# Graph-attention sums in six banks: wide products, a split pair end and values made one tile at a time

## The chip, the cores and the metric

The kernel runs on one NeuronCore of one Trainium2 chip. The metric is the device time in microseconds (us) of one execution; most executions of one kernel agree within 0.3%. The time before is 3559.61 us, median of 3 runs (3555.86 to 3563.96). A run is called slow when it is over 1.5% above the fastest of its kernel; none told of here is.

## The reference, cut to what matters

4096 nodes with 256 features pass two graph-attention layers and then one masked transformer layer. Only the graph-attention layers are touched:

```python
def _gat_layer(x, adj_mat, W, a):                 # 8 heads of 32
    Wh = jnp.einsum('nd,hdo->hno', x, W)
    src = jnp.einsum('hno,ho->hn', Wh, a[:, :O])
    dst = jnp.einsum('hno,ho->hn', Wh, a[:, O:])
    e = jax.nn.leaky_relu(src[:, :, None] + dst[:, None, :], 0.2)
    e = jnp.where(adj_mat[None, :, :] > 0, e, NEG_INF)
    alpha = jax.nn.softmax(e, axis=-1)
    return jnp.einsum('hnm,hmo->hno', alpha, Wh)   # then transposed and reshaped
```

The exponential of a leaky ReLU of a sum is one of two products, depending on the sign of the sum. So the kernel needs no exponential per edge. It compares (a 0/1 matrix `t8` per head, already ANDed with the mask) and sums two kinds of value rows: with `t8`, and with the mask alone.

## The kernel before

Work goes by layer, block of node tiles (4, 4, 8, 8, 8 tiles of 128 nodes in layer 0, then 8, 8, 8, 8), pair of heads (4) and group of sources (8 groups of 4 tiles). The code numbers the source groups by `q` and calls them quarters, though there are eight. Each value is held as two float16 halves, a high and a low one. `V1` is 33 (32 features and the denominator), `VW` 66, `SW` 198. A node tile needs 198 columns: 66 for each head and 66 for the mask. The sums are added up in PSUM, the memory that TensorE writes, of which the kernel uses eight banks. Two tiles share a bank, so eight tiles take four banks; two more are the buffer `two` for the values, and two are `turn` banks.

```python
for n in range(TILES[l][nb]):
    w, at = n // per, slice(n % per * P, (n % per + 1) * P)
    sums = acc[n // 2][:, n % 2 * SW : (n % 2 + 1) * SW]
    for m in range(G):
        for j in range(2):                 # head
            for k in range(2):             # high half, low half, onto the same 66 columns
                nc.tensor.matmul(sums[:, j * VW : (j + 1) * VW], t8[:, j, w, m, at],
                                 vst[g][:, m, 2 * p + j, k * VW : (k + 1) * VW], ...)
        for k in range(2):                 # mask, both heads
            nc.tensor.matmul(sums[:, 2 * VW :]..., masks[l, nb][g][:, w, m, at],
                             vst[g][:, m, 2 * p : 2 * p + 2, k * VW + V1 : (k + 1) * VW], ...)
    if g == NG - 1 and n % 2 == 1:
        nc.scalar.copy(ev[:, n - 1 : n + 1]..., acc[n // 2][:, : 2 * SW])
# ... (cut)
def values(l, q, half):                    # two node tiles at a time
    pv = two_banks()                       # one buffer of two banks
    # ... 4 float32 matmuls; negd, r, tops; for i in range(2): exp, product, high half, low half
```

In the profiles TensorE is PE, and its weight loads are PEld. ScalarE (ACT) and VectorE (DVE) share the comparisons, DVE does the AND. `compare` for group i + 2 is issued before the matmuls of group i. In layer 0, `mask_turn` also reads rows of the adjacency matrix into one of three row buffers (`g_rows`), converts them on DVE (`adj_bf`), transposes them on TensorE into a `turn` bank and copies them out on ACT. `features` loads rows of x into the same `g_rows` buffers and transposes them through `turn` too.

Of the kernel before, what the change touches and what calls it, by code (L numbers as in the profile page):

```python
# [8 lines left out]
F32 = mybir.dt.float32  # L9
# [6 lines left out]
AF = mybir.ActivationFunctionType  # L16
ALU = mybir.AluOpType
AX = mybir.AxisListType
# [3 lines left out]
P = 128  # L22
BIG = 2.0**100
LRELU = 0.2
# [657 lines left out]
VALUE_MAX = 12.0  # L682
# [66 lines left out]
def graph_attention(  # L749
# [16 lines left out]



    nc = tc.nc
    N = adj.shape[0]  # L770
    H, D, O = weights[0][0].shape
# [10 lines left out]
    NG = NT // G  # L782
    V1 = O + 1
    VW = 2 * V1
    SW = 3 * VW

    dram = ctx.enter_context(tc.tile_pool(name="g_dram", bufs=1, space=DRAM))
    s_d = [dram.tile([H, N], F32, name=f"s_d{l}") for l in range(NL)]
# [14 lines left out]
    make_identity(nc, ident_f)  # L803

    vst = [keep.tile([P, G, H, 2 * VW], F16, name=f"vst{q}") for q in range(NG)]

    def two_banks():
        return ps.tile([P, 2, 512], F32, name="two")

    def turn_bank(shape, dtype):  # L810
        return ps.tile(shape, dtype, name="turn", tag="turn", bufs=2)
# [66 lines left out]
    for l, (w, a) in enumerate(weights):  # L878
        L = Layer()
        L.w_ext = keep.tile([P, DC, D + 2 * H], F32, name=f"g_w_ext{l}")  # L880
        for c in range(DC):
            nc.sync.dma_start(
                L.w_ext[:, c, 0:D].rearrange("p (h o) -> p h o", o=O),
                w[:, c * P : (c + 1) * P, :].rearrange("h p o -> p h o"),
            )
        a_sb = rows_p.tile([P, H, 2, O], F32, name="g_rows")
        nc.sync.dma_start(
            a_sb.rearrange("p h s o -> p (h s o)"), spread(a, [[0, P], [1, H * 2 * O]])
        )
        wa = rows_p.tile([P, H, O], F32, name="g_rows")  # L890
        for c in range(DC):
            for s in range(2):
                nc.vector.tensor_tensor(
                    wa,
                    L.w_ext[:, c, 0:D].rearrange("p (h o) -> p h o", o=O),
                    a_sb[:, :, s, :],
                    op=ALU.mult,
                )
                nc.vector.tensor_reduce(
                    L.w_ext[:, c, D + s * H : D + (s + 1) * H], wa, AX.X, ALU.add  # L900
                )
        L.negd = keep.tile([P, NT, H], F32, name=f"g_negd{l}")
        L.r = keep.tile([P, NT, H], F32, name=f"g_r{l}")
        L.tops = keep.tile([P, NG, 2], F32, name=f"g_tops{l}")
        L.ft = {}
        layers.append(L)

# [14 lines left out]
    def term_rows(l, q):  # L922

        L = layers[l]
        pr = turn_bank([P, HB], F32)
        for c in range(DC):
            nc.tensor.matmul(
                pr[:H, :],
                L.w_ext[:, c, D : D + H],
                L.ft[q][:, c, :],  # L930
                start=(c == 0),
                stop=(c == DC - 1),
            )
        sr = rows_p.tile([H, HB], F32, name="g_rows")
        nc.scalar.copy(sr, pr[:H, :])
        nc.sync.dma_start(s_d[l][:, q * HB : (q + 1) * HB], sr)

    def values(l, q, half):

        L = layers[l]  # L940
        pv = two_banks()
        for i in range(2):
            t = 2 * half + i
            for c in range(DC):
                nc.tensor.matmul(  # L945
                    pv[:, i, : D + 2 * H],
                    L.ft[q][:, c, t * P : (t + 1) * P],
                    L.w_ext[:, c, :],
                    start=(c == 0),
                    stop=(c == DC - 1),  # L950
                )
        at = slice(G * q + 2 * half, G * q + 2 * half + 2)
        nc.vector.tensor_scalar(
            L.negd[:, at, :], pv[:, :, D + H : D + 2 * H], -1.0, None, op0=ALU.mult
        )
        nc.scalar.activation(L.r[:, at, :], pv[:, :, D : D + H], AF.Exp, scale=LRELU - 1.0)
        nc.vector.tensor_reduce(
            L.tops[:, q, half : half + 1], pv[:, :, :D], AX.XY, ALU.max, apply_absolute_value=True
        )
        heads = vst[q][:, 2 * half : 2 * half + 2].rearrange("p t h v -> p (t h) v")  # L960
        for i in range(2):

            big = some.tile([P, 2, H], F32, name="g_big")
            nc.scalar.activation(big, L.negd[:, at, :], AF.Exp, scale=(-1.0, -LRELU)[i])
            prod = some.tile([P, 2, H, V1], F32, name="g_prod")
            nc.vector.tensor_scalar(prod[:, :, :, O], big, UP, None, op0=ALU.mult)
            nc.vector.tensor_tensor(
                prod[:, :, :, :O],
                pv[:, :, :D].rearrange("p t (h o) -> p t h o", o=O),
                prod[:, :, :, O : O + 1].to_broadcast([P, 2, H, O]),  # L970
                op=ALU.mult,
            )
            part = prod.rearrange("p t h v -> p (t h) v")
            high = heads[:, :, i * V1 : (i + 1) * V1]
            low = heads[:, :, VW + i * V1 : VW + (i + 1) * V1]
            nc.scalar.copy(high, part)
            nc.vector.tensor_tensor(low, part, high, op=ALU.subtract)

    def check_values(l):
        L = layers[l]  # L980
        for values_, bound in (
            (L.tops.rearrange("p q t -> p (q t)"), VALUE_MAX),
            (L.negd.rearrange("p t h -> p (t h)"), DST_MAX),
            (L.r.rearrange("p t h -> p (t h)"), R_MAX),
        ):
            checks.below(some, values_, bound)

    def preparation(l, q):

        steps = [lambda: (term_rows(l, q), values(l, q, 0)), lambda: values(l, q, 1)]  # L990
        if q + 1 < NG:
            steps.insert(0, lambda: features(l, q + 1))
        else:
            steps.append(lambda: check_values(l))
        return steps
# [39 lines left out]
    def pair_end(l, nb, p, ev):  # L1035
# [5 lines left out]
        cols = slice(2 * p * O, (2 * p + 2) * O)  # L1041
        held = {}
        wide = [P, n, 2, V1]

        def block(name, last):
            return ep.tile([P, BT, 2, last], F32, name=name)[:, :n]

        def sums(i):

            return ev[:, :n, 0 : 2 * VW].rearrange("p t (j v) -> p t j v", j=2)[  # L1050
                :, :, :, i * V1 : (i + 1) * V1
            ]

        def step_load():
            held["x"] = block("e_x", O)
# [1 line left out]

        def step_sum():
            y = block("e_y", V1)
            over = ev[:, :n, 2 * VW :].rearrange("p t (j v) -> p t j v", j=2)  # L1060
            nc.vector.tensor_tensor(y, over, sums(1), op=ALU.subtract)
            nc.vector.tensor_tensor(  # L1062
                y, y, L.r[:, at, 2 * p : 2 * p + 2].unsqueeze(3).to_broadcast(wide), op=ALU.mult
            )
            nc.vector.tensor_tensor(y, y, sums(0), op=ALU.add)
            held["y"] = y

        def step_divide():
# [87 lines left out]
    for i, (l, nb, p, g) in enumerate(groups):  # L1156
# [30 lines left out]
        if not (i + 2 < len(groups) and groups[i + 2][1:] in ((0, 0, 0), (0, 0, 1))):  # L1187
            prepare(i + 2)
        t8 = s8.pop(i)
        if g == 0:  # L1190
            acc = [
                ps.tile([P, 512], F32, name=f"bank{k}") for k in range(TILES[l][nb] // 2)
            ]
        if g == NG - 1:
            ev = ep.tile([P, BT, SW], F32, name="ev")
        for n in range(TILES[l][nb]):
            w, at = n // per, slice(n % per * P, (n % per + 1) * P)
            sums = acc[n // 2][:, n % 2 * SW : (n % 2 + 1) * SW]
            for m in range(G):
                first, last = g == 0 and m == 0 and n % 2 == 0, g == NG - 1 and m == G - 1  # L1200
                for j in range(2):
                    for k in range(2):
                        nc.tensor.matmul(  # L1203
                            sums[:, j * VW : (j + 1) * VW],
                            t8[:, j, w, m, at],
                            vst[g][:, m, 2 * p + j, k * VW : (k + 1) * VW],
                            start=first and j == 0 and k == 0,
                            stop=False,
                        )
                for k in range(2):  # L1210
                    nc.tensor.matmul(  # L1211
                        sums[:, 2 * VW :].rearrange("p (j v) -> p j v", j=2),
                        masks[l, nb][g][:, w, m, at],
                        vst[g][:, m, 2 * p : 2 * p + 2, k * VW + V1 : (k + 1) * VW],
                        start=False,
                        stop=last and k == 1 and n % 2 == 1,
                    )
            if g == NG - 1 and n % 2 == 1:
                nc.scalar.copy(
                    ev[:, n - 1 : n + 1].rearrange("p t v -> p (t v)"), acc[n // 2][:, : 2 * SW]  # L1220
                )
            if slots:
                slots.pop(0)()
        while slots:
# [508 lines left out]
```

## Time and profile before

| stretch (from the first sum matmul of a pair of heads to that of the next) | us |
|---|---|
| until the first sum matmul | 47.4 |
| first pair of layer 0 (makes five of eight quarters of the values) | 81.9 |
| the other 7 four-tile pairs | 213.3 |
| layer 0, blocks 2 and 3 (8 pairs, with mask turns) | 429.8 |
| layer 0, last block (4 pairs; holds the start of layer 1) | 230.0 |
| first pair of layer 1 | 86.1 |
| the other 15 pairs of layer 1 | 732.4 |
| end of the graph layers | 1820.8 |
| transformer | 1741 |

The cuts are read from the start times of the sum matmuls in the trace; the graph layers end with the last of them. A clean pair is a pair of eight tiles beside which neither mask tiles are turned nor values made. A "unit" is what one node tile does with one 128-row of sources; 256 units make a pair of eight tiles. A step is the time from one matmul's start to the next one's start. The lines behind the table are shown in the prediction. One more matters for what follows. It is the view of the sums' banks: what had the matmuls idle before them (us, times).

```profile
its engine sat idle before it (us, times) until:
  PE bank L1211: 25.1, 9
  issue: 23.5, 28
  ACT ev L1219: 7.0, 6
```

"Issue" is time in which an engine waited for nothing that the profile shows: 28 waits before sum matmuls, 23.5 us.

### The profile page before, as it was taken

To read this page: it belongs to the slowest core of one execution; us is meant where nothing else is said; L and a number is where in the kernel's file an instruction comes from. 1 tells how busy PE (TensorE), PEld (TensorE's weight loads), DVE (VectorE), ACT (ScalarE), POOL (GpSimd) and SP (SyncE) were. 2 spreads that over 40 slices of the span, in tenths; PEclk is the share of its full clock that TensorE was granted. 3 is DMA by queue.
4 is the path that set the end of the run, shared out by engine and by line. 5 is a ranking of instruction groups with operands and counts; after the bars stand their busy time and mean duration, and the time that the engine had idled before them with its cause. 6 is when DMAs were issued, how large, how long until landed. Compare 5 with 4: busy or idle time off the path is not lost.

```text
span 3561.9 us, 131329 instructions
## 1 busy us (share of the span) xinstructions
PE 3392.7 (95%) x60099; PEld 2180.5 (61%) x60099; DVE 2857.7 (80%) x3344; ACT 2681.5 (75%) x3176; POOL 1239.4 (35%) x538
## 2 busy tenths in 40 slices
PE   7898999999989999999987999999999999997998
PEld 5898999999969999999964111111111111122666
DVE  7999788888798888888852999999999999996111
ACT  5899898988668888888854777777777777775332
POOL 0000000000000000000000999999999999996110
PEclk9999999999999999999998999999999999998999
DMA  5566554531211212111147010101010110002110
GB/s 174 169 195 210 160 163 135 160 102 39 75 50 37 83 40 75 39 57 46 28 103 194 13 43 16 40 13 37 19 31 25 25 36 13 25 10 69 42 48 25
DMA packets 199685, 254.84 MB, mean 72 GB/s; under 512 B 88080, under 2 KB 134672, under 8 KB 199120
## 3 DMA queue, kind: packets, MB, share of 16 engines
q1 hardware_dynamic: 199120, 246.34, 23.1%
q8 instruction: 472, 7.73, 0.9%
q14 instruction: 93, 0.76, 0.1%
HBM read 203.83 MB, written 42.47 MB: 69 GB/s over the span
## 4 chain that ended last, share of the span: by engine, by line
PE 77%; DVE 8%; ACT 7%; issue 3%; POOL 2%; DMA 2%; SPq 0%; DVEq 0%; ACTq 0%; POOLq 0%
PE bank L1203 26%; PE bank L1211 13%; PE u_ps L1452 11%; PE u_av L1466 11%; PE u_dn L1466 5%; DVE u_e L1461 4%; ACT t L1025 3%; PE misc L1638 3%; POOL u_both L1552 2%; PE misc L1391 2%; ACT u_ps L1459 1%; PE two L945 1%; PE misc L1622 1%; ACT stage L851 1%; PE turn L850 1%
## 5 line engine op out<-in xcount | busy, mean ns | idle before, releaser
L1203 PE MATMUL bank<-vst,t 128*128 128x66 f16 x32768 | 1567.9, 194 | 29.2 <-issue 15.2
L1203 PEld LDWEIGHTS <-t 128*128 128x128 fp8e4 x32768 | 1554.3, 98 | 38.5 <-issue 30.0
L1211 PE MATMUL bank<-vst,mask 128*128 128x66 f16 x16384 | 1554.6, 193 | 8.5 <-issue 8.3
L1025 ACT ACTIVATE t<-s_b,g_negd 128x1024 int8<-128x1024 f32 (+1 forms) x1296 | 1266.2, 1048 | 212.4 <-PE bank L1203 198.5
L1552 POOL TENSOR_TENSOR u_both<-u_e 128x1024 f32<-128x1024 f32 x512 | 1200.2, 2369 | 241.1 <-DVE u_e L1461 240.9
L1461 DVE SCALAR_TENSOR_TENSOR u_e<-u_mask,u_ps 128x1024 f32<-128x1024 uint8 x1024 | 1201.7, 1215 | 100.8 <-ACT u_ps L1459 95.5
L1459 ACT ACTIVATE u_ps<-u_ps 128x1024 f32<-128x1024 f32 x1024 | 1010.7, 1008 | 296.0 <-PE u_ps L1452 277.0
L1211 PEld LDWEIGHTS <-mask 128*128 128x128 fp8e4 x16384 | 1048.8, 97 | 11.1 <-issue 10.2
L1030 DVE TENSOR_TENSOR t<-t,mask 128x2048 int32<-128x2048 int32 (+1 forms) x288 | 590.7, 2052 | 210.9 <-ACT t L1025 204.8
L1027 DVE TENSOR_SCALAR t<-s_b,g_negd 128x1024 fp8e4<-128x1024 f32 (+1 forms) x1008 | 635.3, 688 | 10.1 <-PE bank L1203 9.3
masks.py:197 POOL MEMSET u_ident<- 128x128 f32 x1 | 0.2, 205 | 1821.5 <-DVE e_y L1062 1821.5
L1452 PE MATMUL u_ps<-u_q,u_k 128*128 128x512 f16 x2048 | 580.3, 384 | 36.8 <-DMA u_q<-half_d 21.6
L1452 PEld LDWEIGHTS <-u_k 128*128 128x128 f16 x2048 | 139.3, 97 | 743.7 <-issue 685.4
L1466 PE MATMUL u_av<-u_e,u_v 128*32 128x512 f32 x4096 | 547.2, 605 | 0.1
L1466 PE MATMUL u_dn<-u_both,u_ones 128*32 128x512 f32 x2048 | 274.0, 605 | 1.3 <-POOL u_both L1552 1.3
L1466 PEld LDWEIGHTS u_av<-u_e,u_v 128*32 128x32 f32 x4096 | 80.8, 108 | 219.2 <-issue 211.0
L1629 ACT ACTIVATE u_hid<-misc,u_b 128x512 f32<-128x512 f32 x64 | 42.4, 684 | 142.7 <-PE misc L1622 142.7
L851 ACT ACTIVATE stage<-turn 128x1024 fp8e4<-128x1024 bf16 x112 | 112.2, 1018 | 0.0
L1645 DVE TENSOR_TENSOR u_xres<-u_xres,misc 128x256 f32<-128x256 f32 x32 | 13.5, 421 | 122.7 <-PE misc L1638 122.7
L1638 PE MATMUL misc<-u_w,u_hid 128*128 128x256 f32 x512 | 111.8, 379 | 0.0
L1622 PE MATMUL misc<-ln_cols,u_w 128*128 128x512 f32 x256 | 111.2, 592 | 0.0
L1466 PEld LDWEIGHTS u_dn<-u_both,u_ones 128*32 128x32 f32 x2048 | 40.6, 108 | 110.9 <-issue 108.4
(100 smaller groups left out, 1565.9 us busy)
## 6 DMA issues: line engine op xcount, KB each, us to landing
g_rows<-in_adj_dram SPq DMA_DIRECT2D x128, 512.0 KB
mask<-mask SPq DMA_DIRECT2D x120, 256.0 KB
s_b<-s_d SPq DMA_DIRECT2D x56, 512.0 KB
u_mask<-mask SPq DMA_DIRECT2D x32, 512.0 KB
mask<-stage SPq DMA_DIRECT2D x28, 512.0 KB
half_d<-u_halves SPq DMA_DIRECT2D x32, 256.0 KB
u_k<-half_d SPq DMA_DIRECT2D x32, 256.0 KB
u_q<-half_d SPq DMA_DIRECT2D x32, 256.0 KB
```

The source lines that it names most:

```text
L851: nc.scalar.activation(staged[0].rearrange("p i g n -> p (i g) n")[:, :, t * P : (t + 1) * P], pt, AF.Identity, saturate=False,)
L1025: nc.scalar.activation(to.bitcast(I8), s, AF.Sign, bias=negd, scale=-1.0)
L1027: nc.vector.tensor_scalar(to, s, negd, None, op0=ALU.is_ge, saturate=False)
L1030: nc.vector.tensor_tensor(both, both, mask.unsqueeze(1).to_broadcast(list(both.shape)), op=ALU.bitwise_and)
L1203: nc.tensor.matmul(sums[:, j * VW : (j + 1) * VW], t8[:, j, w, m, at], vst[g][:, m, 2 * p + j, k * VW : (k + 1) * VW], start=first and j = ...
L1211: nc.tensor.matmul(sums[:, 2 * VW :].rearrange("p (j v) -> p j v", j=2), masks[l, nb][g][:, w, m, at], vst[g][:, m, 2 * p : 2 * p + 2, k * ...
L1452: nc.tensor.matmul(ps[:, j, :], k_st[:, h, mt * P : (mt + 1) * P], q_st[:, h, :], start=True, stop=True,)
L1459: nc.scalar.activation(ps, ps, AF.Exp, scale=SCALE)
L1461: nc.vector.scalar_tensor_tensor(e, mask, 0.0, ps, op0=ALU.not_equal, op1=ALU.mult)
L1466: nc.tensor.matmul(to[j * O : (j + 1) * O, :], lefts[j], es[j // 2][:, j % 2, :], start=start, stop=stop,)
L1552: nc.gpsimd.tensor_tensor(both, es_of[i - 1][u], es_of[i][u], op=ALU.add)
L1638: nc.tensor.matmul(po[:, :D], hid[:, f, at : at + P], w2_sb[:, f, :], start=(f == 0), stop=(f == FC - 1),)
```

## The change

The intent is fewer matmul instructions for the same columns. The two halves of the first head are no longer added in PSUM but stand side by side, as do those of the mask: 132 columns in one matmul. The second head still adds in place (two of 66). So a unit is 132, 66, 66, 132 and no longer six times 66. A tile now needs 330 columns, eight tiles six banks, and the value buffer loses its two: values are made one tile at a time in the `turn` banks. The pair end has to add the halves.

```diff
-    def values(l, q, half):
+    def values(l, q, t):
-        pv = two_banks()
+        pv = turn_bank([P, 512], F32)
... (the same steps for one tile; both products in one operation)
         def step_sum():
+            halves = ev[0][:, : 2 * n]
+            nc.vector.tensor_tensor(
+                halves[:, :, :VW], halves[:, :, :VW], halves[:, :, VW:], op=ALU.add
+            )
... (one subtraction and one addition of 528 become two each of 264)
-            acc = [ps.tile([P, 512], F32, name=f"bank{k}") for k in range(TILES[l][nb] // 2)]
+            banks = -(-2 * tiles // 3)
+            acc = [ps.tile([P, 512], F32, name=f"bank{k}") for k in range(banks)]
... (places: three wide sums and one narrow one to a bank)
+                todo = [
+                    (k_0, acc[k_0][:, o_0 : o_0 + 2 * VW], s_of_m[0], heads[:, 0, :]),
+                    (k_1, acc[k_1][:, o_1 : o_1 + VW], s_of_m[1], heads[:, 1, :VW]),
+                    (k_1, acc[k_1][:, o_1 : o_1 + VW], s_of_m[1], heads[:, 1, VW:]),
+                    (k_m, acc[k_m][:, o_m : o_m + 2 * VW]..., masks[l, nb][g][:, w, m, at], over),
+                ]
... (two copies a bank: wide sums to ev_broad, narrow ones to ev_narrow)
```

## The prediction

> **What bounds the kernel now.** I read the page first (who is busy, what the chain is made of), then the groups by line, then the busy time of each engine in stretches cut at the points where one pair of heads ends and the next begins, and last the matmuls one by one.
>
> ```profile
> span 3561.9 us, 131329 instructions
> ...
> PE 3392.7 (95%) x60099; PEld 2180.5 (61%) x60099; DVE 2857.7 (80%) x3344; ACT 2681.5 (75%) x3176; POOL 1239.4 (35%) x538
> ...
> PE bank L1203 26%; PE bank L1211 13%; PE u_ps L1452 11%; PE u_av L1466 11%; PE u_dn L1466 5%; DVE u_e L1461 4%; ACT t L1025 3%; PE misc L1638 3%; POOL u_both L1552 2%; PE misc L1391 2%; ACT u_ps L1459 1%; PE two L945 1%; PE misc L1622 1%; ACT stage L851 1%; PE turn L850 1%
> ...
> L1203 PE MATMUL bank<-vst,t 128*128 128x66 f16 x32768 | 1567.9, 194 | 29.2 <-issue 15.2
> ...
> L1211 PE MATMUL bank<-vst,mask 128*128 128x66 f16 x16384 | 1554.6, 193 | 8.5 <-issue 8.3
> ```
>
> The chain of waits puts 26% + 13% = 39% of the span (1389 us) on the two matmul lines that the change touches. All of that lies in the two graph-attention layers, which end at 1821 us (start of the last L1203 matmul); the transformer after it, 1741 us, is not touched. 1389 us / 49152 = 28.3 ns, but the chain leaves pieces out; the stretches give a better figure. In them each engine has its busy time and its count of instructions:
>
> ```profile
> 820.50:868.70 48.20, 48.20 (x1541) 48.20 (x1538) 41.34 (x47) 40.23 (x42) 0.00 (x0) 1.00 0.12 36
> ...
> 669.30:721.90 52.60, 52.42 (x1613) 52.32 (x1611) 47.02 (x57) 48.83 (x52) 0.00 (x0) 1.00 0.51 162
> 247.50:279.00 31.50, 29.84 (x850) 28.97 (x850) 28.64 (x56) 31.43 (x49) 0.00 (x0) 1.00 0.79 259
> 1002.40:1088.50 86.10, 81.08 (x1663) 68.18 (x1662) 77.33 (x132) 61.86 (x107) 0.00 (x0) 1.00 0.09 28
> ```
>
> The columns are length, PE, PEld, DVE, ACT, POOL, granted clock, DMA. Four kinds of stretch:
> - A clean pair of heads in a block of eight node tiles (first line): PE never idles, 1536 sum matmuls in 48.2 us. DVE 41.3, ACT 40.2. PE-bound. Of 36 pairs, 19 are like this or nearly: four in layer 0's last block, 15 in layer 1. Cut in the same way, the 15 last 48.2 to 51.1 us, so about 0.4 us each is lost to other waits (most of it named "issue").
> - Layer 0's blocks 2 and 3 (second line), which also turn mask tiles: 8 pairs of 50.5 to 60.4 us. PE has 48.1 us of sums and 72 transposes of 56 ns, ACT 48.8.
> - Four-tile pairs (third line), 7 of them, about 26 to 32 us: ACT 31.4 of 31.5. ACT-bound; PE has only 24.1 us of sums.
> - The first pair of each layer (fourth line), where values are made: DVE 77.3 of 86.1.
>
> Matmul by matmul in a clean pair:
>
> ```profile
> 1399.81 0.29 PE L1203 MATMUL bank<-vst,t 128*128 128x66 f16 x4
> 1399.94 0.22 PE L1211 MATMUL bank<-vst,mask 128*128 128x66 f16 x2
> 1400.00 0.29 PE L1203 MATMUL bank<-vst,t 128*128 128x66 f16 x4
> 1400.13 0.22 PE L1211 MATMUL bank<-vst,mask 128*128 128x66 f16 x2
> 1400.19 0.29 PE L1203 MATMUL bank<-vst,t 128*128 128x66 f16 x4
> ```
>
> One unit (a node tile by one 128-row of sources) repeats every 0.19 us. From the start times in the trace its six steps are 29, 34, 33, 32, 30 and 30 ns (medians over layer 1), together 188. 256 units make 48.1 us.
>
> **What the Trainium skill says.** (1) "TensorE: Matmul & The Clock Gate", section "Back-to-back issue gap": a warm isolated gap is about N/2.4 + 2.5 ns. For 66 columns that is 30.0 and the mask matmuls step by 30; for 128 it is 55.8 and the mask transposes step by 56; for 512 it is 215.8 and L1452's shortest steps are 215 to 216. The trace agrees. The same section's ~81 ns for a stream of load and matmul at 128 does not show here. (2) "PSUM — Partial Sum Buffer", section "The four PSUM rules": a first matmul clears the accumulate bits of the whole bank, so a bank may be opened only once; the changed code opens each once. No run here shows it yet. (3) "VectorE: DVE Perf Modes", section "The TRN2 errata": a float32 tensor_tensor takes (N+151)/0.96 ns. For 528 that is 707 and for 264 432; the e_y rows have 702 to 707 and 426 to 430. Agrees, so I use it for the new sizes.
>
> **The change, part by part.**
>
> *Sums.* Per unit six matmuls of 66 columns become 132, 66, 66, 132. Columns stay at 396, so only the fixed part of two matmuls goes. By N/2.4 + 2.5: 2 x 57.5 + 2 x 30 = 175 ns. Today's unit is 8 ns above its own 180 (the steps around matmuls of a head's own products, 32 to 34); I keep half of that, as half of those matmuls remain narrow: 179. Saved 188 - 179 = 9 ns a unit, 256 x 9 = 2.3 us a clean pair (48.1 to 45.8). Over all 8192 units 74 us, if PE were the bound everywhere.
>
> *Evacuation.* Eight tiles: four copies of 396 (483 ns each, 1.93 us) become five of 396, one of 132, five of 66, one of 198. From 483 ns for 396 and 372 for 256 (another copy row) the slope is 0.8 and the fixed part near 0.16: 5 x 0.483 + 0.26 + 5 x 0.21 + 0.32 = 4.05 us. ACT +2.1 us a pair; for four tiles +1.05.
>
> *Pair end.* Three DVE operations of 528 (2.1 us) become one of 1056 ((1056+151)/0.96 = 1.26 us), four of 264 (0.43 each) and one of 528 (0.71): 3.7 us. DVE +1.6 us; four tiles +1.0.
>
> *Values by one tile.* Per two tiles DVE had 0.17 + 0.69 + 2 x (0.17 + 0.68 + 0.70) = 4.0 us; now twice (0.15 + 0.42 + 0.32 + 0.68 + 0.70), 4.5. ACT goes from 1.9 to about 2.4. But the two-bank buffer had no second copy: the timeline before layer 1 shows one half every 5 us or so, for 4 us of DVE work. Two turn banks let the next tile's matmuls run beside it.
>
> **What lies on the path.** In a clean pair PE remains the longest, but thinly: 45.8 against DVE 41.4 + 1.6 = 43.0 and ACT 40.2 + 2.1 = 42.3. The pair end is a burst: banks 4 and 5 close only with the last tile, and the copies end about 1.5 us after it, against 0.5. ACT then owes two or three groups of comparisons (4 or 5 x 1.06 us each, then DVE's 2.29 us AND) with two groups (11.4 us) of buffers ahead. Laying it out by hand, the slack goes from about 4 us to about 1, and DVE's longer pair end can use that up; I charge 0.7 us a pair. Net 48.9 to 46.9, 19 x 2.0 = -38 us. Blocks 2 and 3: PE 45.8 + 4.0, ACT 48.5 + 2.1 = 50.6, so ACT becomes the bound: -1.2 x 8 = -10. Four-tile pairs: ACT already the bound, +1.05 less some of PE's relief: +0.7 x 7 = +5. First pairs: DVE five quarters x 1.0 + 1.6, less what the buffer gives back: +4 for both layers. Tails of the two layers (last copies, longer sum): 2 x 2.2 = +4. Sum -35: 3559.6 - 35 = 3525 us.
>
> **Rivals.**
> - *ACT or DVE takes over in the clean pairs.* For it: 43.0 and 42.3 of 45.8, ANDs that wait for ACT, bursts at pair ends. Against: today's clean pairs show no idle PE at all. If it costs 2 us a pair more, the gain is gone: about 3555 to 3560.
> - *PE gains more.* For it: the extra 8 ns may come from weight loads that follow each other every 30 ns, and these become rarer (four a unit for six); fewer instructions to fetch may also remove "issue" waits. At 175 ns a unit with no stall: 19 x 3.7 + 8 x 2 = 86, about 3475. Against: the burst at the pair's end.
> - *Wide matmuls gain nothing.* If the mask matmul with four runs of 33 reads more slowly, or the 132-column product steps at two times 32, a unit stays near 184 and the extra copies show: about 3555 to 3570. Against: today's mask matmul with two runs of 33 is among the fastest.
> - *Start of a layer.* Values now share the two turn banks with features, term rows and mask turns; if they queue there, +10 us.
>
> **Range and chances.** The sure part is 4 ns to 13 ns a unit in 27 pairs (28 to 90 us); what is uncertain is what the bursts give back (10 to 60). 8 in 10: 3487 to 3557. Over 2% faster needs below 3488, so nearly no stall: 0.11. Over 2% slower would need 71 us more, a new wait in every pair: 0.02.
>
> **What would show it.** Right: steps of about 57 ns after 132-column matmuls and units of 177 to 181; clean pairs of 46 to 47.5 us; ACT's copies near 4 us a pair; the DVE add near 1.26 us; four-tile pairs a little longer; the transformer unchanged. Wrong: units of 184 or more; PE idle over 2 us in each clean pair on the AND or on a comparison; first pairs of a layer changed by over 10 us either way.

## The result, and the profile after

The changed kernel takes 3523.55 us (median of 4, 3520.12 to 3526.0), beside 3561.78 us for the kernel before in the same rounds. The ratio is 0.9894, 95% interval 0.9876 to 0.9911. A ratio here is the mean time of one kernel's fast runs over that of the other's in the same rounds, so it is not quite the ratio of the medians. By the 2% rule of the record this counts as "same", though the interval lies below 1. The record has no mark of correctness for this run; the seven experiments are all marked correct.

The page of the changed kernel (span, busy time, chain of waits, costliest groups):

```profile
span 3524.0 us, 99099 instructions
...
PE 3357.4 (95%) x43715; PEld 2128.8 (60%) x43715; DVE 2903.2 (82%) x3580; ACT 2730.9 (77%) x3528; POOL 1239.1 (35%) x538
...
PE bank L1234 34%; PE u_ps L1480 12%; PE u_av L1494 11%; PE u_dn L1494 6%; ACT t L1021 5%; DVE u_e L1489 4%; PE misc L1666 3%; PE misc L1419 2%; POOL u_both L1580 2%; DVE t L1023 1%; ACT u_ps L1487 1%; ACT stage L850 1%; DVE t L1026 1%; PE misc L1650 1%; PE turn L926 1%
...
L1234 PE MATMUL bank<-vst,mask 128*128 128x132 f16 x8192 | 1503.5, 222 | 0.0
```

There are 32768 sum matmuls where there were 49152, and they hold 34% of the span on the chain, not 39%. ACT and DVE did not shrink: DVE is 45.5 and ACT 49.4 us busier.

The stretches, in the same columns as before (length, PE, PEld, DVE, ACT, POOL, clock, DMA): a clean pair, a pair of block 3, a four-tile pair, the first pair of layer 1 and the first pair of layer 0.

```profile
820.90:867.60 46.70, 46.70 (x1025) 46.57 (x1025) 42.59 (x50) 41.40 (x50) 0.00 (x0) 1.00 0.13 37
675.20:726.50 51.30, 51.23 (x1100) 50.79 (x1098) 47.90 (x60) 49.99 (x60) 0.00 (x0) 1.00 0.53 162
274.30:307.10 32.80, 29.84 (x590) 29.22 (x590) 29.28 (x59) 32.07 (x53) 0.00 (x0) 0.95 0.73 227
997.40:1082.00 84.60, 82.78 (x1160) 67.72 (x1161) 80.82 (x181) 68.29 (x145) 0.00 (x0) 1.00 0.09 28
51.20:155.50 104.30, 84.15 (x784) 60.58 (x785) 74.91 (x201) 67.25 (x166) 0.00 (x0) 0.88 0.37 118
```

The last of these before the change:

```profile
47.40:129.30 81.90, 71.49 (x1026) 54.52 (x1025) 71.24 (x149) 60.06 (x122) 0.00 (x0) 0.94 0.48 155
```

A clean pair goes from 48.2 to 46.7 us and PE's busy time still fills it. But the first pair of layer 0 grows by 22.4 us, and DVE did only 3.7 us more work in it: the rest is waiting.

| stretch | before | after | difference | the prediction's step |
|---|---|---|---|---|
| until the first sum matmul | 47.4 | 51.2 | +3.8 | in "first pairs" |
| first pair of layer 0 | 81.9 | 104.3 | +22.4 | first pairs, both layers: +4 |
| 7 four-tile pairs | 213.3 | 213.1 | -0.2 | +5 |
| blocks 2 and 3 | 429.8 | 405.6 | -24.2 | -10 |
| last block of layer 0, with the start of layer 1 | 230.0 | 223.1 | -6.9 | 4 of the 19 clean pairs, one tail |
| first pair of layer 1 | 86.1 | 84.7 | -1.4 | in "first pairs" |
| 15 pairs of layer 1 | 732.4 | 701.6 | -30.8 | 15 of the 19 clean pairs |
| end of the graph layers | 1820.8 | 1783.6 | -37.2 | -35 in all |

The total is almost as predicted, but two of its terms are far off. The experiments ask why.

The idle time before the sums' matmuls, in the same view of the banks as before:

```profile
its engine sat idle before it (us, times) until:
  PE bank L1234: 19.8, 7
  DVE t L1026: 15.5, 10
  ACT ev_narrow L1246: 6.3, 7
```

The "issue" waits are gone. The groups by shape give the pieces of the longer evacuation, the copying of the sums out of PSUM, and of the pair end (columns: shapes, count, busy us, mean ns, idle before):

```profile
L1240 ACT COPY ev_broad<-bank 128x396 f32<-128x396 f32 x156 | 77.0, 506 | 18.7 <-PE bank L1234 18.2
L1246 ACT COPY ev_narrow<-bank 128x66 f32<-128x66 f32 x156 | 37.9, 243 | 0.0
...
L1053 DVE TENSOR_TENSOR ev_broad<-ev_broad 128x1056 f32<-128x1056 f32 x28 | 35.0, 1251 | 21.2 <-ACT ev_broad L1240 21.2
```

The DVE add is 1251 ns where 1257 was worked out. The narrow copies are 243 ns where I had 0.21 us, and the wide ones 506 where I had 483. At the end of the pairs of layer 1 ACT goes straight from a comparison to the copy of the first bank, about 0.6 us before the next pair begins, and that pair waits for the bank. At one such border (ACT's narrow copy of the first bank, then the first matmul of the next pair):

```profile
1222.14 0.21 ACT L1246 COPY ev_narrow<-bank 128x66 f32<-128x66 f32 x1
...
1222.40 0.22 PE L1234 MATMUL bank<-vst,t 128*128 128x132 f16 x1
```

At each of the 15 borders after layer 1's first pair, the first matmul starts 42 to 43 ns after that copy has ended, and 196 to 226 ns after the matmul before it, where that step is 59 ns elsewhere. So the border costs 0.14 to 0.17 us a pair. PE's busy column hides this, since the modelled ends of the matmuls reach past it. In the kernel before that step is 30 ns, as everywhere.

Where the 22 us of the first pair went shows in its chain of waits (start us, us, what):

```profile
66.88 0.61 DVE adj_bf L844
...
67.53 0.57 DVE vst L972
68.10 0.60 DVE adj_bf L844
...
68.73 5.08 DMA g_rows<-in_x_dram
...
73.94 1.94 PE turn L916 x8
```

In this chain the load of the next rows of x starts only when DVE has converted a row of the adjacency matrix, since that frees a row buffer. Then come 5.08 us of transfer, the transposes, the term rows and the values, and DVE idles meanwhile (start us, us, engine, line, operation, and in brackets the idle time before):

```profile
71.62 0.69 DVE L844 TENSOR_SCALAR adj_bf<-g_rows 128x1024 bf16<-128x1024 int32 x1
81.05 0.17 DVE L950 TENSOR_SCALAR g_negd<-turn 128x8 f32<-128x8 f32 x1 [8.75 <-PE turn L942]
```

The pair's chain has two such loads, of 5.08 and 5.29 us, and DVE idles 5.93, 8.75, 1.37, 7.55 and 3.02 us before the values of its five quarters. Before the change the pair's chain has one, of 4.62 us. It starts 10.3 us into the pair, the first one after the change 17.5 us. DVE does not wait before the conversion that this one needs; the conversion stands behind other work. In DVE's timeline before the change conversions (`adj_bf`) stand between the operations of the values (`g_prod`, `vst`); after it the first one stands behind nearly all those of a quarter's four tiles. First a piece before, then one after:

```profile
54.78 0.68 DVE L845 TENSOR_SCALAR adj_bf<-g_rows 128x1024 bf16<-128x1024 int32 x1
55.38 1.28 DVE L967 TENSOR_TENSOR g_prod<-two,g_prod 128x512 f32<-128x512 f32 x2
```

```profile
66.18 0.69 DVE L972 TENSOR_TENSOR vst<-g_prod,vst 128x528 f16<-128x528 f32 x1
66.80 0.68 DVE L844 TENSOR_SCALAR adj_bf<-g_rows 128x1024 bf16<-128x1024 int32 x1
```

### The profile page after: what moved, and what is told of

Same layout as the page of the kernel before. It is cut to its first block, busy times and chain, and to the rows that moved or that the text cites. A ratio compares the mean times of both kernels' runs of the same rounds, so it can differ in the third digit from the quotient of the medians.

```text
span 3524.0 us, 99099 instructions
## 1 busy us (share of the span) xinstructions
PE 3357.4 (95%) x43715; PEld 2128.8 (60%) x43715; DVE 2903.2 (82%) x3580; ACT 2730.9 (77%) x3528; POOL 1239.1 (35%) x538
## 4 chain that ended last, share of the span: by engine, by line
PE 73%; DVE 11%; ACT 9%; DMA 3%; issue 2%; POOL 2%; SPq 0%; DVEq 0%; ACTq 0%; POOLq 0%
PE bank L1234 34%; PE u_ps L1480 12%; PE u_av L1494 11%; PE u_dn L1494 6%; ACT t L1021 5%; DVE u_e L1489 4%; PE misc L1666 3%; PE misc L1419 2%; POOL u_both L1580 2%; DVE t L1023 1%; ACT u_ps L1487 1%; ACT stage L850 1%; DVE t L1026 1%; PE misc L1650 1%; PE turn L926 1%
## 5 line engine op out<-in xcount | busy, mean ns | idle before, releaser
L1234 PE MATMUL bank<-vst,t 128*128 128x66 f16 (+1 forms) x24576 | 1517.9, 203 | 22.0 <-DVE t L1026 15.5
L1234 PEld LDWEIGHTS <-t 128*128 128x128 fp8e4 x24576 | 1505.6, 97 | 33.2 <-DVE t L1026 18.0
L1234 PE MATMUL bank<-vst,mask 128*128 128x132 f16 x8192 | 1503.5, 222 | 0.0
L1234 PEld LDWEIGHTS <-mask 128*128 128x128 fp8e4 x8192 | 803.6, 98 | 1.9 <-issue 0.9
```

What stands on the lines that cost most here:

```text
L1234: nc.tensor.matmul(to, left, right, start=k not in opened, stop=last)
```

## The experiments

The theory was that the values, now in the turn banks, hold up the mask turns and features that use the same banks (T). The rivals were that the halved operations cost the time (H), that the shared row buffers do (X), and that the new sums or their evacuation do (S). Four kernels were run together in three rounds beside the kernel before (median 3567.27 us on that chip), then three more (3560.96 us there). Medians of different calls are not quite comparable, ratios are.

**Values alone.** The kernel before, with `values` as in the changed kernel:

```diff
-        pv = two_banks()                      # one call per two tiles
+        pv = turn_bank([P, 512], F32)         # one call per tile; sums unchanged
```

> The kernel before with one part of the change alone: values made one node tile at a time in the two turn banks (the two-bank buffer is gone), sums as before with six matmuls of 66 columns. In the profile of the changed kernel layer 0's first pair lasts 104.3 us where it lasted 81.9, and starts at 51.2 us instead of 47.4. Theory T (the values' part causes this, since its tiles hold the turn banks that mask turns and features need): first pair 100 to 106 us, start near 51, layer 1 as before, so about 3560 + 26 = 3586 us, ratio near 1.007. Rival S (the new sums or their evacuation disturb the first pair): the first pair stays within 3 us of 82 and the time within 6 us of before.

Measured: 3592.49 us, ratio 1.0068 (1.0051 to 1.0085). The first pair:

```profile
50.70:152.80 102.10, 83.86 (x1040) 62.03 (x1041) 75.03 (x201) 66.72 (x163) 0.00 (x0) 0.89 0.38 122
```

It lasts 102.1 us and starts at 50.7. The graph layers end at 1850.0 us, 29.2 later. The loss belongs to the values' part; S falls. So does the later start, 3.3 of the 3.8 us. Against T's "layer 1 as before", layer 1's first pair also grew, by 3.0 us; the 15 pairs after it (732.7 us) did not change.

**Own banks for the values of layer 0.** The four-tile blocks use banks 0 to 2 only:

```diff
-        pv = turn_bank([P, 512], F32)
+        pv = (
+            ps.tile([P, 512], F32, name=f"bank{3 + t % 3}") if l == 0 else turn_bank([P, 512], F32)
+        )
```

> The changed kernel, but in layer 0 the values of a node tile go to one of the banks 3, 4 and 5, which its four-tile blocks don't use; mask turns, features and term rows have the turn banks to themselves. Theory T (queue in the turn banks): the first pair returns to 82 us or less from 104, the span loses 20 to 28 us, about 3500. Rival H (halving itself, more and shorter instructions on DVE and ACT, costs the time): first pair stays above 97, span within 6 us of 3523. Rival X (the load of x waits for a row buffer that DVE frees late, whatever the banks): between, 90 to 100 us.

Measured: 3498.83 us, ratio 0.9813 (0.9797 to 0.9829).

```profile
51.60:125.90 74.30, 66.67 (x742) 52.00 (x742) 66.61 (x176) 57.53 (x143) 0.00 (x0) 0.94 0.48 152
```

The first pair is 74.3 us, shorter than the 81.9 of the kernel before. H falls for this pair: the same halved operations do not lengthen it once they have room. T's figure is met. The values have three banks here, one more than the buffer `two` had, so this shows what room gives, not what two banks of their own would. The other stretches are those of the changed kernel within 1 us. So the start stays late (51.6 us), and which part of the values delays it is not settled.

**Own buffer for the rows of x of layer 0.** The evacuation tile is idle in the first pair:

```diff
-        x_nat = rows_p.tile([P, G, D], F32, name="g_rows")
+        if l == 0:
+            x_nat = ep.tile([P, 2 * BT, 2 * VW], F32, name="ev_broad")
+            x_nat = x_nat.rearrange("p s v -> p (s v)")[:, : G * D].rearrange("p (t d) -> p t d", d=D)
+        else:
+            x_nat = rows_p.tile([P, G, D], F32, name="g_rows")
```

> The changed kernel, but in layer 0 the rows of x are loaded into the evacuation tile, which is idle in the first pair, and not into one of the three row buffers that the adjacency rows use; banks as in the changed kernel. In the chain of the first pair the load of x (about 5 us, three times) follows a mask conversion on DVE that frees a row buffer. Rival X (that wait is the loss): the first pair falls to 85 to 90 us and the span by 14 to 20 us, about 3506. Theory T (turn banks are the cause, the late load a consequence of them): the pair keeps at least 97 us and the span falls by less than 8 us.

Measured: 3508.27 us, ratio 0.9835 (0.9818 to 0.9851).

```profile
55.80:138.20 82.40, 71.02 (x766) 53.59 (x765) 73.28 (x197) 64.95 (x160) 0.00 (x0) 0.96 0.44 143
```

The first pair falls to 82.4 us, and the first sum matmul comes 4.6 us later (55.8), probably since all loads of x now go through one tile. The first pair is below X's 85 to 90 us and far from T's 97. Together with the run before it, neither theory is right alone: separate banks for the values, or a separate buffer for x, each take most of the loss away. Counted to the end of the first pair, which the change had put off by 26.2 us, own banks give back all of it (125.9 us) and the own buffer 17.3 (138.2). The last link is shown: the conversion ends late, the load of x waits for its row buffer, and 5 us of transfer lie open. How the shared banks make the conversion late is argued only in part. In the first pair of the changed kernel the mask's transposes do wait for a bank that holds values:

```profile
PE turn L849 <- DVE g_prod L963: 2.8, 3, 1.1
```

But that is 2.8 us in three waits, the first of them ending at 99.8 us, and the conversions before both loads follow other DVE work without a pause. What put them behind the values in DVE's order no run shows. With own banks they stand between the values again; with the own buffer for x they stay behind them, and the load no longer needs them.

**Narrow matmuls apart.**

```diff
+                    (k_1, acc[k_1][:, o_1 : o_1 + VW], s_of_m[1], heads[:, 1, :VW]),
                     (k_0, acc[k_0][:, o_0 : o_0 + 2 * VW], s_of_m[0], heads[:, 0, :]),
-                    (k_1, acc[k_1][:, o_1 : o_1 + VW], s_of_m[1], heads[:, 1, :VW]),
                     (k_1, acc[k_1][:, o_1 : o_1 + VW], s_of_m[1], heads[:, 1, VW:]),
                     (k_m, ...mask...),
```

> The changed kernel with another order of the four matmuls in a unit: second head high, first head wide, second head low, mask wide, so that no two narrow ones follow each other. Today the steps are 57, 33, 33, 59 ns, 182 a unit. Theory W (narrow matmuls in a row are slowed by weight loads that come every 30 ns): 30 + 57.5 + 30 + 57.5 = 175 to 177 a unit, clean pairs about 45 us, 30 to 45 us less in all unless ACT or DVE take over, 3480 to 3495. Rival (the extra nanoseconds belong to a matmul's own operands or to the change of bank, whatever the order): 180 to 184 a unit, time within 6 us of 3523.

Measured: 3508.56 us, ratio 0.984 (0.9823 to 0.9856). A clean pair:

```profile
1258.80:1305.00 46.20, 46.11 (x1025) 45.98 (x1025) 42.60 (x50) 41.41 (x50) 0.00 (x0) 1.00 0.14 37
```

The unit is 179 ns by the median, 180 by the mean, with steps of 29, 57, 33 and 60 ns (57, 33, 33, 59 before). So neither side is right in full. The narrow matmul that follows the mask's now steps by 29 to 30, as W expected, but the one before the mask still takes 33, and the mask's step does not shrink. Order matters for 3 of the 7 ns above the prediction's estimate of 175; what the other 4 are stays open. The mean is above the median chiefly because of one step a pair, the border shown above: here the first matmul of a new pair comes 294 to 299 ns after the one before it and not 60, and 41 to 43 ns after ACT's narrow copy of the first bank. So what shows there is the pair end's copies on ACT; the run with six matmuls told of next has the same copies and no such step (30 ns).

**Six matmuls in six banks.**

```diff
-   (k_0, acc[k_0][:, o_0 : o_0 + 2 * VW], s_of_m[0], heads[:, 0, :]),
+   (k_0, acc[k_0][:, o_0 : o_0 + VW], s_of_m[0], heads[:, 0, :VW]),
+   (k_0, acc[k_0][:, o_0 + VW : o_0 + 2 * VW], s_of_m[0], heads[:, 0, VW:]),
... (the mask's product cut in two in the same way; places, copies, pair end and values unchanged)
```

> The changed kernel with its six banks, copies, pair end and values, but each 132-column matmul cut into two of 66 again, so six matmuls a unit as before. Theory F (a fixed cost per matmul is the whole gain of the sums): the unit returns from 182 to 187 to 189 ns, clean pairs from 46.7 to 48.2 us, layer 1 after its first pair from 702 to 723 us. Theory I (the waits that the profile of before names issue, about 6 us in layer 1 and more in blocks 2 and 3, come with the number of instructions): these waits return too, layer 1 after its first pair near 730, blocks 2 and 3 together from 406 to 428 us or more, the whole 3570 to 3585. Rival (the waits went for another reason, the bank layout or the copies): PE idle stays near nothing in layer 1, the whole near 3555 to 3565.

Measured: 3586.67 us, ratio 1.0076 (1.0058 to 1.0094). A clean pair of it, then the idle time before the sums:

```profile
1309.00:1357.20 48.20, 48.20 (x1541) 48.20 (x1538) 42.55 (x50) 41.48 (x50) 0.00 (x0) 1.00 0.13 37
```

```profile
its engine sat idle before it (us, times) until:
  PE bank L1238: 21.3, 8
  issue: 20.2, 26
```

The unit is back at 188 ns with the same six steps as in the kernel before, within 1 ns, so the whole gain a unit is the two matmuls fewer. The 15 pairs of layer 1 take 725.5 us, nearer F's 723 than I's 730; blocks 2 and 3 take 432.0 us, I's "428 us or more". The whole is 1.7 us above I's range and far from the rival's 3555 to 3565. The "issue" waits are back, 26 of them, 20.2 us, but not everywhere. Cut by time, before 342 us, from 342 to 900 and after 1080 us, the kernel before has 5.1, 11.6 and 6.8 us of them, this one 4.7, 14.5 and 1.0, the changed kernel none. So I holds for layer 0. In layer 1 the waits mostly stayed away with six matmuls too. The run with the values alone has 6.2 us of them there, so the values are not the reason.

The traces that were kept also tell what these waits are. (This was counted over their records; `prof` has no view of it.) Number PE's instructions in order, weight loads included. Then all 28 of the waits in the kernel before stand at place 193 or 194 in a run of 256, and so do the 26 of this run and the 28 of the run with the values alone. The page of the kernel before, then that of the changed one, list the 16 KB packets of the instruction queue:

```profile
q8 instruction: 472, 7.73, 0.9%
```

```profile
q8 instruction: 344, 5.64, 0.7%
```

That is about one packet for every 256 of PE's instructions (120198 before, 87430 after; 472 again in this run). Each of the waits ends 1.0 to 1.6 us after such a packet has landed. So PE waits there for its next block of instructions. From 1080 us on, 256 instructions last 4.0 us at six matmuls a unit and 5.8 at four, and their packet lands a median 2.3 us (kernel before), 2.6 (this run) or 4.8 (changed kernel) before the place; the least is 1.3, 1.0 and 4.1. With fewer instructions each packet has time to spare. Why the packets come a little earlier in layer 1 of this run than in the kernel before, at the same count, is open; the bank layout, the copies or chance are left.

**Both improvements, then a third.** Own banks and narrow matmuls apart; then also the rows of x of quarters 3 to 7 in the evacuation tile (`if l == 0 and q >= 3`).

> The changed kernel with both improvements: layer 0's values in the banks 3 to 5 and the narrow matmuls kept apart. They gained 24.7 and 15.0 us alone in the medians. The first acts only in the first pair, the second in pairs where PE is the bound, so they should add: 3484 us, 3480 to 3488. If it stays above 3492, one of them hid behind something that the other also removes.

Measured: 3476.67 us, ratio 0.9764 (0.9748 to 0.978). That is below the range given in us, which ignored that the chips differ (the kernel before is 6.3 us faster on this one). In ratios the two should give 0.9813 x 0.984 / 0.9894 = 0.976, and do: they add.

> As the run with both improvements, and the rows of x for quarters 3 to 7 of layer 0 go into the idle evacuation tile (the first three quarters keep the row buffers, since loading all of them through one tile delayed the first sum matmul from 51.2 to 55.8 us). If the wait for a row buffer is only a consequence of the queue in the turn banks, nothing more is won: within 3 us of the run with two improvements. If it still holds up features in the first pair, up to 6 us less.

Measured: 3472.03 us, ratio 0.9752 (0.9735 to 0.9768), correct, and the fastest of all. It gains 4.6 us, inside the second expectation's "up to 6". Its first pair:

```profile
47.40:120.20 72.80, 65.50 (x743) 49.88 (x742) 70.50 (x187) 59.07 (x151) 0.00 (x0) 0.95 0.48 149
```

The first sum matmul and the pair together end at 120.2 us, and at 120.0 (50.7 + 69.3) in the run with two improvements. So the gain is not in the first pair, where it was looked for; the 7 pairs after it take 212.4 us and not 215.3. The graph layers of the two profiled executions end only 2.8 us apart, and the transformer, which the edit does not touch, differs by 4.8. So what was predicted is not shown, and the 2.8 us in the 7 pairs are unexplained and may be chance.

## Why the prediction was right, and where it was not

The time came out 1.5 us from the predicted one and far inside the range. By its own steps:

- *"PE-bound" in the clean pairs, and columns kept while two matmuls' fixed part goes*: right. Putting the two matmuls back restores 188 ns.
- *"I keep half of that ... 179. Saved 9 ns a unit"*: mis-sized. Nearly all of the excess stayed, 182 against 175, the estimate by the formula; 6 ns were saved. With another order of the four, 179 is reached.
- *"I charge 0.7 us a pair" for the burst at the pair's end*: right in kind, mis-sized: the border costs 0.14 to 0.17 us. DVE grew by 1.2 us and ACT by 1.2 us of busy time, less than the 1.6 and 2.1 worked out. Clean pairs came to 46.7 us, where I had 45.8 + 0.7 and about 0.4 of other waits, 46.9: two errors that cancel. The sum itself was uneven. 48.9 to 46.9 is 2.0, but the parts give only 2.3 - 0.7 = 1.6; the rest comes from taking more other waits before (48.9 is about the measured mean, 48.8) than the 0.4 stated and kept after. With 1.6 the total would have been about 3532 us. And one of the 19 pairs is not clean: the last of layer 0 holds the start of layer 1 and lasts 85.4 us.
- *Waits named "issue"*: I had them stay, as part of both figures. They went entirely: 6.8 us in layer 1, whose 15 pairs therefore gained 30.8 us though the unit alone gives 15 x 256 x 6 ns = 23 us, and 16.7 us in layer 0. Six matmuls bring them back, nearly all of them in layer 0. They were waits for blocks of instructions; the prediction names fewer instructions to fetch as a reason why they might go, under the rival "PE gains more".
- *"Blocks 2 and 3 ... ACT becomes the bound: -1.2 x 8 = -10"*: mis-sized by 14 us. (The figures beside it, 48.1 + 4.0 before and 50.6 after, give 1.5, not 1.2.) PE and ACT both measure close to the pair's length after (51.2 and 50.0 of 51.3), so PE stayed in the bound, and the stretch from 342 to 900 us lost 11.6 us of "issue" waits that I had not counted on losing. The six-matmul run gives all of it back (432.0 us), so it came from fewer matmuls.
- *"Four-tile pairs +5"*: -0.2 measured. Four of the seven became 0.5 to 1.4 us longer, as reckoned, but the last became 2.8 us shorter, which I have not traced.
- *"First pairs ... +4 for both layers"*: wrong in kind and size. I took it that two turn banks give back time because the next tile's matmuls run beside DVE. Layer 1 became 1.4 us shorter, but not for that reason: with six matmuls the values by one tile make its first pair 3.0 us longer (values alone; 2.9 in the run with six banks). In layer 0 the pair grew by 22.4 us and started 3.8 later, with the values in the banks that the mask turns also use. It was listed as the rival "start of a layer", with 10 us, and not followed to the row buffer and the load of x behind it. "First pairs of a layer changed by over 10 us" was one of the prediction's own signs of being wrong, and it came true; the unit of 182 ns lies just outside its sign of being right, 177 to 181.

So the total was that close by luck: an error of 21 us in the first pairs was met by 14 us in blocks 2 and 3, 5 in the four-tile pairs, and smaller differences elsewhere. The mechanism of the main part was right, that of the values was not.

## What to carry to other kernels

When a buffer of its own is dissolved into a shared pool, follow every other user of that pool to what it frees next: here a conversion came later, a row buffer came free later, and a 5 us load lay open. Own banks or an own buffer took most of that away. Where PE is the bound on narrow matmuls, count instructions as well as columns, and try their order; if "issue" waits stand at a fixed distance in instructions, suspect their fetching. And compare by stretches even when the total agrees with the forecast: a loss of 26 us in layer 0's start lay hidden in a net gain of 37, and undoing it, with the new order, took the ratio from 0.989 to 0.976.

## What the Trainium skill lacked or had wrong

- "TensorE: Matmul & The Clock Gate", "Back-to-back issue gap": the section's sustained ~81 ns a matmul at 128 columns does not hold here: the mask transposes step by 56 ns, each with its own weight load. The other formula, N/2.4 + 2.5, comes out low for a unit: 188 ns measured against 180 for six matmuls, 182 against 175 for four. No page gives a figure for the order of wide and narrow matmuls: 182 or 179 ns for the same four.
- "Runtime: NRT & Kernel Launch", "Instruction fetch mechanics", says that instruction fetch is hidden behind the issue of instructions. Here it is not always hidden: 28 waits before sum matmuls (23.5 us), all at one place in a run of 256 PE instructions, are gone when the instructions fall from 131329 to 99099, and 26 of them (20.2 us) are back at 131888. How long they are is not explained by the count alone (in layer 1 6.8 us before, 1.0 us at 131888).
- "VectorE: DVE Perf Modes", "The TRN2 errata": the page has (N+151)/0.96 as exact at 512 and 2048. It is within 2% at 1056 (1257 ns, measured 1251) and 264 (432, measured 425 to 431), but 3% high at 132 (295, measured 286). The page's row for ScalarE from PSUM, (172+N)/1.2, is low for these copies: 198 ns for 66 columns, measured 243 by the mean, and 0.21 to 0.29 us one after another in one pair end.
